# Attention and gated feed-forward on one core: both parts of the weighted sums of a head group issued together

## The chip, the cores and the metric

The kernel runs on one core of a Trainium2 chip. The metric is the device time of one execution in microseconds (us); for the kernel before, three executions were timed. Engines are named as in the profile: PE (matmuls), PEld (its weight loads), DVE (vector engine), ACT (scalar engine), POOL, and SP, which here only issues DMAs.

## The reference

32 sequences of 256 tokens with 128 features pass through attention with 16 heads of 8 features, a residual and a layer norm, then a gated feed-forward net with a hidden width of 512, a residual and a layer norm.

```python
scores = jnp.einsum('bhid,bhjd->bhij', Q, K) / jnp.sqrt(jnp.float32(hd))
delta = t[:, None] - t[None, :]
decay = jnp.where(delta < 0, 0.0, -delta.astype(jnp.float32))
scores = jnp.where(delta < 0, -jnp.inf, scores) + decay
out = jnp.einsum('bhij,bhjd->bhid', softmax(scores), V)      # then @ Wo.T + bo
x = layernorm(x + attention)

h = silu(x @ w1.T * s1) * (x @ w2.T * s2)
h = gelu(h @ h1.T * sh1)
h = gelu(h @ h2.T * sh2)
x = layernorm(x + h @ w3.T * s3)
```

Everything is float32. The entries of the five weight matrices are small whole numbers times a scale per output.

## The kernel before

**Pairs and steps.** Two sequences (512 tokens) form a pair; there are 16 pairs, 0 to 15. `step(n)` (L713) does the attention weights of pair n. Woven into it are the row maxima of pair n+1, the projections of pair n+2, the end of the feed-forward net of pair n-2, and, in the second half of the step, the feed-forward net of pair n-1 (`feed`, L558).

**Places.** The first half of a step is a loop over twelve places, i = 0 to 11 (L721). The 16 heads are four groups of four, and each group owns three places. At the first two of a group, `weigh` (L429) computes scores of two heads for all queries against the first 128 keys; at the third, scores of all four heads for the second 128 keys against the second 128 queries (tiles with a d in the name, s_1d for group 1). ACT takes the exponential of each score tile into a tile e, and POOL puts zeros above the diagonal (L462). At the same place `row_maxima` (L370) computes score tiles of the next pair, PE adds the causal mask to them with four small bf16 matmuls (s<-tri_q,ident_b), and DVE reduces them to maxima m. In the profile a `weigh` tile reads s<-qs,ks (64 rows) and a `row_maxima` tile s<-ks,qs (62 rows).

**Score tiles in PSUM.** `two` (L288) gives tiles of two banks from a pool of three, used for the scores of `weigh` and `row_maxima` and for the gates and hidden layers. A tile can be written again when its reader (ACT's exponential, DVE's reduction, a gate's product) is done. `work` (L285) gives tiles of one bank from a pool of two.

**Weighted sums.** `outputs(n, a)` (L469) is a generator for group a: 16 matmul records over 256 columns (jc = 0, first 128 keys) and 16 over 128 columns (jc = 1, second 128 keys) accumulate into the tile pa, in packets of four for the four column strips of the array. pa takes two groups; after the second group ACT copies it to oT, PE transposes it (pt), and DVE divides by the sums (rec, on). Each `next` of the generator runs it to its next `yield`. It is made at the third place of its group, so its first `next` comes at the first place of the next group: jc = 0 at places 3, 6 and 9, jc = 1 at 4, 7 and 10, each behind the place's score tiles (L728), and oT at 7, the transposition at 8. After `outputs` of a place come, by place, a transposition of the normed x of pair n-1 (px1T, place 9) or a part of the projections (pxT at 1, pq at 3, pk at 5, each of which ACT and DVE split into a high and a low half: qhi, qlo, khi, klo).

**Gates.** The fourth group's generator runs in the second half. `feed` yields after each of its four gates: a gate is four matmuls into one tile (pw), a SiLU on ACT (sg), a product on DVE (h0w), its rounded copy (a CAST, h) and the rest as a low half, which POOL computes for the first two gates and DVE for the other two. At each yield `rest` (L749) takes one step: before the change the first three are jc = 0, then jc = 1 with oT, then the transposition; the fourth runs the transposition of the maxima (pm) and the division. Then come two hidden layers (podd, peven), whose matmuls take the halves of h in the order of the gates.

**Order.** PE, DVE, ACT and SP keep the order in which the program calls them (`InOrder`, L50); nothing is reordered by cost. The pools decide only which tile a new one takes, and so what it waits for.

Of the kernel before, what the change touches and what calls it, by code (L numbers as in the profile page):

```python
# [33 lines left out]
G, C = 4, 4  # L34
# [27 lines left out]
def tile_attn_ffn(  # L62
# [96 lines left out]
    def prepare(func):  # L159

        act.activation(nothing, half[:, 0:1], func)
# [123 lines left out]
    def work(nm):  # L285
        return ps_w.tile([P, 512], F32, name=nm, tag="work")
# [179 lines left out]
        es.append(e)  # L466


    def outputs(n, a):  # L469
        v = pairs[n]["v"]  # L470
        *first, second = pairs[n][("e", a)]
        r, e = divmod(a, 2)
        if e == 0:
            pairs[n]["pa"] = work(f"pa_{n}_{r}").rearrange("c (b i) -> c b i", b=2)
        pa = pairs[n]["pa"]
        for jc in range(2):
            for b in range(2):
                for c in range(C):
                    h, p = c // 2, c % 2
                    at = VSLOT * (C * r + c) + VHEAD * e  # L480
                    pe.matmul(
                        pa[32 * c : 32 * (c + 1), b, jc * P :],
                        lhsT=v[:, 2 * b + jc, at : at + 32],
                        rhs=second[:, p, h, b, :] if jc else first[h][:, p, b, :],
                        start=(e == b == jc == 0), stop=(e == b == jc == 1),
                        tile_position=(0, 32 * c),
                    )
            if jc == 0:
                yield
        if e == 0:  # L490
            return
        oT = op.tile([P, TOK], F32, name=f"oT_{n}_{r}", tag="oT", bufs=1)
        act.copy(oT, pa.rearrange("c b i -> c (b i)"))
        yield

        if r == 0:
            pairs[n]["on"] = op.tile([P, NT, D], F32, name=f"on_{n}", tag="on", bufs=1)
        on = pairs[n]["on"].rearrange("i t (r e c d) -> i t r e c d", r=2, e=2, c=C)
        po = work(f"pt_{n}_{r}").rearrange("i (t c k) -> i t c k", t=NT, c=C)
        for t in range(NT):  # L500
            pe.transpose(po[:, t].rearrange("i c k -> i (c k)"), oT[:, t * P : (t + 1) * P], ident)
        yield
        rec = mp.tile([P, NT, C, 2], F32, name=f"rec_{n}_{r}", tag="rec")
        vec.reciprocal(rec, po[:, :, :, HD : HD + VHEAD + 1 : VHEAD])
        for e in range(2):
            vec.tensor_tensor(
                on[:, :, r, e], po[:, :, :, VHEAD * e : VHEAD * e + HD],
                rec[:, :, :, e : e + 1].to_broadcast([P, NT, C, HD]), ALU.mult,
            )
# [19 lines left out]
    def first_norm(n):  # L529
        x1 = x1s[n % 3]  # L530
        yield from layernorm(pairs[n]["xb"], x1, f"a_{n}")
        pairs[n] = dict(x1=x1)
# [4 lines left out]
    def turn(n, exact):  # L537
        pt = work(f"px1T_{n}")
        for t in range(NT):
            pe.transpose(pt[:, t * P : (t + 1) * P], pairs[n]["x1"][:, t, :], ident)  # L540
        x1T = xtp.tile([P, 2, TOK], F32R, name=f"x1T_{n}", tag="x1T")
        if exact:
            act.copy(x1T[:, 0, :], pt)
            vec.tensor_tensor(x1T[:, 1, :], pt, x1T[:, 0, :].bitcast(F32), ALU.subtract)
        else:
            x1T = x1T.bitcast(F32)
            vec.tensor_copy(x1T[:, 0, :], pt)
        pairs[n]["x1T"] = x1T
# [72 lines left out]
    def inexact_weights():  # L621

        found = const.tile([P, 11], F32, name="found")
        at = 0
        for nm, *_ in layers:
            rows = [t[nm].rearrange("p k o -> p (k o)") for t in (loaded, near)]
            for c in range(0, rows[0].shape[1], HID):
                whole, part = (t[:, c : c + HID] for t in rows)
                act.copy(part, whole)
                differ = once.tile([P, HID], F32, name=f"differ_{at}", tag="differ")  # L630
                vec.scalar_tensor_tensor(
                    differ, whole, 1.0, part.bitcast(F32), ALU.mult, ALU.not_equal,
                    accum_out=found[:, at : at + 1],
                )
                at += 1
                yield
        ones_col = const.tile([P, 1], F32, name="ones_col")
        nc.gpsimd.memset(ones_col, 1.0)
        count = work("pcount")
        pe.matmul(count[0:1, 0:11], lhsT=ones_col, rhs=found, start=True, stop=True)  # L640
        total = const.tile([1, 1], F32, name="total")
        vec.tensor_reduce(total, count[0:1, 0:11], AX.X, ALU.add)
        number = const.tile([1, 1], I32, name="number")
        vec.tensor_copy(number, total)
        pairs["inexact"] = number

    def last(n, exact, ws, gp):
        h = pairs[n]["h"]
        pT = work(f"pw3_{n}")
        for k in range(KC):  # L650
            parts = [h[:, i, k, :] for i in range(2 if exact else 1)]
            product(pT, ws["w3"][:, k, :], parts, k == 0, k == KC - 1)
        yT = gp.tile([P, TOK], F32, name=f"yT_{n}", tag="sg")
        act.activation(yT, pT, AF.Copy, scale=sc["s3"])
        yield
        po = work(f"py_{n}").rearrange("p (t d) -> p t d", d=D)
        for t in range(NT):
            pe.transpose(po[:, t, :], yT[:, t * P : (t + 1) * P], ident)
        y = yp.tile([P, NT, D], F32, name=f"y2_{n}", tag="y")
        vec.tensor_tensor(y, po, pairs[n]["x1"], ALU.add)  # L660
        z = yp.tile([P, NT, D], F32, name=f"z_{n}", tag="z")
        yield
        yield from layernorm(y, z, f"f_{n}")
        sp.dma_start(out=ov[n], in_=z)
        del pairs[n]

    def run(gen):
        for _ in gen:
            pass
# [43 lines left out]
    def step(n, exact=None, ws=None, hp=None, gp=None):  # L713


        side = iter(())
        settling = (
            last(n - 2, exact, ws, gp) if n > 1 else first_norm(0) if n else inexact_weights()
        )
        ahead = project(n + 2) if n + 2 < NPAIR else iter(())  # L720
        for i in range(3 * G):  # L721
            weigh(n, i)
            j = i + {0: LEAD, 1: -LAG}.get(n, 0)
            if n + 1 < NPAIR and 0 <= j < 3 * G:
                row_maxima(n + 1, j)
            if i == 3 and late:
                run(late.pop())
            next(side, None)  # L728
            if n and i == 9:
                turn(n - 1, exact)  # L730
            if i in ((0, 2) if n > 1 else (0, 2, 4, 6)) if n else i < 11:
                next(settling, None)

            if i in ((3, 4, 5) if n == 1 else (1, 3, 5)):
                next(ahead, None)
            if i % 3 == 2:
                run(side)
                side = outputs(n, i // 3)
            if n == 0 and i == 3 * G - LEAD:
                maxima_to_rows(1)  # L740
        if n < 2:
            run(settling)
        run(ahead)
        if n + 2 < NPAIR:
            stack(n + 2, "q")
            stack(n + 2, "k", sp if n else act)


        def rest():  # L749
            for _ in range(3):  # L750
                next(side)
                yield
            if n == 1:
                for i in range(3 * G - LAG, 3 * G):
                    row_maxima(2, i)
                    yield
            if 0 < n < NPAIR - 1:
                maxima_to_rows(n + 1)
            run(side)
            yield  # L760
            if n + 2 < NPAIR:
                project_values(n + 2)
                yield
            last_steps = finish(n)
            next(last_steps)
            yield
            yield from last_steps
            if n:
                yield
                yield from first_norm(n)  # L770
            if n == NPAIR - 1:
                yield
                turn(n, exact)
            if n > 1:
                next(settling)
                late.append(settling)

        if n:
            prepare(AF.Silu)
        due = rest()  # L780
        for _ in feed(n - 1, exact, ws, hp, gp) if n else ():
            next(due, None)
        run(due)
# [84 lines left out]
```

## Time and profile before

| | |
|---|---|
| three timed executions | 823.65, 823.84, 826.28 us; median 823.84 |
| the profiled execution | 828.74 us |
| its span, first to last instruction | 826.8 us |
| mean granted PE clock | 0.969 |
| instructions | 17426 |
| PE, groups over pa | 1024 matmul records over the 256-column tiles, 379 ns median; 4 x 256 over 128 columns, 273 ns |

The page gives the busy time of each engine and the chain of work that ended last. Matmul records overlap, so their durations are longer than their distance in time: how long a group holds PE is read from start to start. In the chain the lengths of neighbouring groups add up to time. A single engine's timeline gives the start, the length and, in brackets, the idle time before it with what ended it. In a list of stretches the columns after the length are the busy times of the engines with their numbers of instructions, then the granted PE clock, the share of the DMA engines, and GB/s.

Steps 2 to 13 repeat alike, one every 47.4 us; step 8 lies between 418 and 465 us. PE's clock was granted at half in stretches within the first 100 us and at the very end.

### The profile page before, as it was taken

The numbers are of one execution on the slowest core, as the hardware profiler recorded it, in microseconds if no ns is written. First come the engines' busy times: TensorE is split into PE (matmuls) and PEld (weight loads), VectorE is DVE, ScalarE is ACT, GpSimd is POOL, SyncE is SP. The second block draws the span as 40 slices with busy tenths as digits, with TensorE's granted clock in tenths as the row PEclk, the third lists the DMA queues.
The fourth block names the chain that finished last, engine by engine and source line by source line (L and its number), as shares of the span: only waits on it lengthen the run. The fifth ranks groups of instructions, "written<-read, shape, count | busy, mean of one in ns | idle before, by whom it ended". The sixth has DMA issues, their size and how long they took to land.

```text
span 826.8 us, 17426 instructions
## 1 busy us (share of the span) xinstructions
PE 788.6 (95%) x7046; PEld 556.4 (67%) x7046; DVE 636.0 (77%) x1245; ACT 527.3 (64%) x719; POOL 259.7 (31%) x340
## 2 busy tenths in 40 slices
PE   5896999999999999999999999999999999999994
PEld 2564576676767667676767767676776767666673
DVE  6786677778888887878888777878888787873674
ACT  5065465766576666667677676657666666758662
POOL 5033322414242432314233341423234242424210
PEclk9569699999999999999999999999999999999998
DMA  6814040311404040230404031040404023000001
GB/s 146 224 49 106 14 104 16 91 29 36 97 14 106 27 103 17 61 72 14 106 27 106 14 90 43 20 111 16 107 26 103 5 52 68 14 4 13 1 13 31
DMA packets 39882, 47.49 MB, mean 57 GB/s; under 512 B 3952, under 2 KB 21616, under 8 KB 39792
## 3 DMA queue, kind: packets, MB, share of 16 engines
q1 hardware_dynamic: 37136, 42.82, 21.7%
q10 hardware_dynamic: 2656, 3.48, 1.9%
q8 instruction: 57, 0.93, 0.5%
q14 instruction: 33, 0.27, 0.1%
HBM read 7.48 MB, written 4.19 MB: 14 GB/s over the span
## 4 chain that ended last, share of the span: by engine, by line
PE 83%; DVE 4%; ACT 3%; issue 1%; DMA 1%; POOL 0%; SPq 0%; ACTq 0%; POOLq 0%; DVEq 0%
PE peven L58 14%; PE podd L58 13%; PE s L58 12%; PE pa L58 11%; PE pw L58 10%; PE s_0d L58 2%; PE s_2d L58 2%; PE s_3d L58 2%; PE s_1d L58 2%; PE po L58 2%; PE pq L58 2%; PE pk L58 2%; PE pt L58 2%; PE pv L58 2%; PE px1T L58 1%; PE py L58 1%
## 5 line engine op out<-in xcount | busy, mean ns | idle before, releaser
L58 DVE TENSOR_REDUCE m<-s 128x4 f32<-128x1024 f32 x128 | 155.6, 1219 | 15.8 <-PE s L58 14.6
L58 ACT ACTIVATE e<-s 128x1024 f32<-128x1024 f32 x128 | 130.7, 1022 | 45.6 <-PE s L58 36.2
L462 POOL TENSOR_SCALAR_AFFINE_SELECT e<-e 128x512 f32<-128x512 f32 x128 | 82.3, 643 | 220.9 <-ACT e L58 192.1
L58 PE MATMUL podd<-h,h_near 128*128 128x512 f32 x512 | 131.4, 403 | 1.0 <-DVE m L58 0.5
L58 PE MATMUL peven<-hodd,h_near 128*128 128x512 f32 x512 | 122.7, 396 | 0.0
L58 PEld LDWEIGHTS peven<-hodd,h_near 128*128 128x128 f32 x512 | 95.7, 187 | 23.4 <-DVE hodd L58 0.3
L58 PEld LDWEIGHTS podd<-h,h_near 128*128 128x128 f32 x512 | 91.7, 188 | 23.2 <-DVE h L58 3.5
L58 ACT ACTIVATE hodd<-podd,sh 128x512 fp32r<-128x512 f32 x64 | 44.0, 688 | 62.9 <-PE podd L58 62.8
L58 PE MATMUL pw<-x1T,w_near 128*128 128x512 f32 x256 | 75.6, 418 | 1.1 <-DVE h0w L58 1.1
L58 PEld LDWEIGHTS s<-qs,ks 64*128 64x128 f32 x512 | 39.3, 190 | 49.3 <-issue 35.8
L273 POOL TENSOR_TENSOR rsa<-rsa,half 128x4 f32<-128x4 f32 x16 | 16.3, 1017 | 176.0 <-DVE rsa L58 176.0
L58 PE MATMUL pa<-e,vaug 128*32 128x256 f32 x1024 | 71.4, 393 | 0.0
L58 DVE SCALAR_TENSOR_TENSOR h0w<-pw,s,sg 128x512 f32<-128x512 f32 x64 | 47.9, 749 | 29.4 <-ACT sg L58 29.4
L58 PE MATMUL s<-qs,ks 64*128 64x256 f32 x512 | 65.8, 337 | 0.7 <-ACT e L58 0.5
L58 DVE TENSOR_TENSOR heven<-evenw,heven 128x512 fp32r<-128x512 f32 x64 | 44.2, 692 | 26.6 <-ACT evenw L58 26.1
L58 ACT ACT_TABLE_LOAD x47 | 60.3, 1283 | 3.4 <-issue 2.6
L58 ACT ACTIVATE sg<-pw,s 128x512 f32<-128x512 f32 x64 | 43.6, 683 | 28.3 <-PE pw L58 27.9
L58 PE MATMUL s<-ks,qs 62*128 62x256 f32 x512 | 57.3, 303 | 3.6 <-ACT e L58 2.4
L58 ACT ACTIVATE heven<-peven,sh 128x512 fp32r<-128x512 f32 x48 | 33.4, 695 | 39.8 <-PE peven L58 39.8
L58 PEld LDWEIGHTS pw<-x1T,w_near 128*128 128x128 f32 x256 | 43.4, 188 | 18.4 <-ACT nothing L58 5.8
L580 POOL TENSOR_TENSOR h<-h0w,h 128x512 fp32r<-128x512 f32 x31 | 40.0, 1290 | 43.5 <-DVE h L58 41.3
L58 DVE TENSOR_TENSOR hodd<-oddw,hodd 128x512 fp32r<-128x512 f32 x64 | 43.8, 684 | 10.9 <-ACT oddw L58 10.8
(147 smaller groups left out, 1418.7 us busy)
## 6 DMA issues: line engine op xcount, KB each, us to landing
qs<-qhi SPq DMA_DIRECT2D x32, 256.0 KB
qs<-qlo SPq DMA_DIRECT2D x32, 256.0 KB
ks<-khi SPq DMA_DIRECT2D x26, 256.0 KB
ks<-klo SPq DMA_DIRECT2D x26, 256.0 KB
x<-in_x_dram SPq DMA_DIRECT2D x16, 256.0 KB
out_dram<-z SPq DMA_DIRECT2D x16, 256.0 KB
ks<-khi ACTq DMA_DIRECT2D x6, 256.0 KB
ks<-klo ACTq DMA_DIRECT2D x6, 256.0 KB
```

What stands on the lines that cost most here:

```text
L58: return lambda *args, **kw: self.tc.keep_in_program_order(call(*args, **kw))
L273: nc.gpsimd.tensor_tensor(rs, rs, half, ALU.pow)
L462: nc.gpsimd.affine_select(out=on_diagonal, in_=on_diagonal, pattern=[[0, on_diagonal.shape[1]], [1, P]], base=0, channel_multiplier=-1, co ...
L580: (nc.gpsimd if o < (1 if final else 2) else vec).tensor_tensor(h[:, 1, o, :], whole, h[:, 0, o, :].bitcast(F32), ALU.subtract)
```

## The change

`outputs` now yields before any matmul instead of between the two parts, so at places 3, 6 and 9 it does nothing, and at 4, 7 and 10 both parts follow each other. For the fourth group (`at_once`) it doesn't yield there: both parts and the copy to oT come between the first two gates, the transposition between the second and the third, and nothing between the third and the fourth. `rest` takes an empty step in its place, so all that follows keeps its yield. pa is still taken from its pool at the first `next`.

```diff
-    def outputs(n, a):
+    def outputs(n, a, at_once=False):
         ...
             pairs[n]["pa"] = work(f"pa_{n}_{r}").rearrange("c (b i) -> c b i", b=2)
         pa = pairs[n]["pa"]
+        if not at_once:
+            yield
         for jc in range(2):
             for b in range(2):
                 for c in range(C):
         ...
-            if jc == 0:
-                yield
         if e == 0:
             return
         oT = op.tile([P, TOK], F32, name=f"oT_{n}_{r}", tag="oT", bufs=1)
         act.copy(oT, pa.rearrange("c b i -> c (b i)"))
         yield
         ...
                 run(side)
-                side = outputs(n, i // 3)
+                side = outputs(n, i // 3, at_once=i == 3 * G - 1)
         ...
         def rest():
-            for _ in range(3):
+            for _ in range(2):
                 next(side)
                 yield
+            yield
             if n == 1:
```

In the order of PE's instructions of a step, places 3, 6 and 9 lose the 256-column group, which stands at 4, 7 and 10 ahead of the 128-column one; pq, the score tiles of place 7 and px1T come directly behind the masks of places 3, 6 and 9. Among the gates the order becomes pw, both parts, pw, pt, pw, pw, pm. On ACT the copy to oT of the fourth group comes ahead of the SiLU of the second gate. DVE, POOL and SP keep their order.

## The prediction

> **What bounds the kernel now.** I read the page first (busy shares and the chain), then a table by stages, then the chain in order of time through one step of the pair loop, then single engines in the places that the change touches. All times are from the one profiled execution.
>
> ```profile
> PE 788.6 (95%) x7046; PEld 556.4 (67%) x7046; DVE 636.0 (77%) x1245; ACT 527.3 (64%) x719; POOL 259.7 (31%) x340
> ...
> PE 83%; DVE 4%; ACT 3%; issue 1%; DMA 1%; POOL 0%; SPq 0%; ACTq 0%; POOLq 0%; DVEq 0%
> ```
>
> ```profile
> 388.00:436.00 48.00, 48.00 (x450) 34.40 (x448) 38.63 (x76) 32.81 (x45) 15.67 (x20) 1.00 0.24 58
> 436.00:484.00 48.00, 48.00 (x449) 34.33 (x448) 38.95 (x76) 32.27 (x45) 16.11 (x21) 1.00 0.24 57
> ```
>
> In the second view the columns are the stretch, its length, then busy time of PE, PEld, DVE, ACT and POOL, the granted clock, and DMA. PE is busy in 48.00 of 48.00 us at full clock from about 148 to 676 us. A step lasts 47.4 us (the khi instructions of successive steps start at 383.742 and 431.135). So every tenth of a microsecond that PE gains or loses in a step counts whole, twelve times over in steps 2 to 13, which repeat to a few nanoseconds. The four other steps are priced apart.
>
> The chain through places 5 to 8 of step 8 (start, length, work):
>
> ```profile
> 428.77 1.27 PE s_1d L58 x20
> 430.04 1.06 PE pk L58 x2
> 431.10 0.85 PE s L58 x12
> 431.95 1.00 PE pa L58 x16
> 432.95 0.85 PE s L58 x12
> 433.81 0.57 PE pa L58 x16
> 434.38 1.27 PE s_2d L58 x20
> ```
>
> Here the 1.00 us of pa stands between the two score blocks of places 6 and 7. Beside it ACT runs, 0.07 us earlier on the clock of the timeline:
>
> ```profile
> 431.13 0.69 ACT L58 ACTIVATE khi<-pk,bk_sb 128x512 fp32r<-128x512 f32 x1 [0.62 <-PE pk L58]
> 431.72 1.02 ACT L58 ACTIVATE e<-s 128x1024 f32<-128x1024 f32 x1
> ```
>
> **The change part by part.** Nothing is added or removed: the same 32 matmul records of each group of four heads (16 over 256 columns, 16 over 128) are issued together. DVE, POOL and SP (and with SP the DMAs) keep their order; on ACT one copy moves (below). Three effects, all on PE.
>
> (1) Places 3/4 and 9/10: one interruption less. Inside the 256-column group the packets of four start 0.216 us apart; the last is followed 0.329 us later by whatever comes next, so leaving costs 0.113. The first packet of the 128-column group takes 0.133 where the next take 0.109, so entering costs 0.024. Joined, the two parts save 0.137. What then follows the masking matmuls (pq at place 3, px1T at 9) starts as it does elsewhere: mask to pxT takes 0.171 and mask to pa 0.170, and a transposition group takes 0.586 after mask and after pa alike. I take −0.137 twice. Bounds: 0, if joining saves nothing, and −0.17, the whole mask step. Waits checked: px1T asks for nothing new, pq waits only for xT, copied by 423.9. The row maxima of place 10 wait for the exponential of place 9, which ends at 437.794; their weight load would be due at 437.83 and can start 0.05 after that end, at 437.84: the cover has run out but costs 0.01.
>
> (2) Places 6/7: a wait takes the place of the cover. The score tiles rotate through three PSUM buffers; the row maxima of place 7 reuse the tile that the exponential of place 6 reads. Before, pa's 1.00 us hid that. Now the block of place 7 starts at 431.88 and its row maxima are due 0.34 later, at 432.22. The exponential still ends at 432.737, since it starts only when khi leaves ACT (0.585 after khi's start, in each of the twelve steps). What such a wait costs is shown at place 1 of every step:
>
> ```profile
> 420.25 1.01 ACT L58 ACTIVATE e<-s 128x1024 f32<-128x1024 f32 x1
> ...
> 421.31 0.30 PEld L58 LDWEIGHTS s<-ks,qs 62*128 62x128 f32 x4
> 421.31 0.50 PE L58 MATMUL s<-ks,qs 62*128 62x256 f32 x4
> ...
> 421.74 0.11 PEld L58 LDWEIGHTS <-ident_b 64*64 64x64 bf16 x4
> ```
>
> The exponential ends at 421.26; the weight load follows 0.05 later and the maxima take 0.43 to the mask instead of 0.33, because the weights too waited. So at place 7: maxima at 432.79, mask 433.22, pa 433.40, both parts 0.888 + 0.550, and s_2d at 434.84 where it stood at 434.309: +0.53 with the saved interruption in it. Behind the wait stand mask, both pa parts and all of place 8, PE being in order. Bounds: +0.43 (no slower restart) and +0.65 (the whole cover of 1.00 lost less the slack of 0.35 that the block itself gives).
>
> The Trainium skill, "TensorE: Matmul & The Clock Gate", Part 3, The mechanism, has PE pull weight loads ahead of matmuls in flight. By it the restart would cost no extra 0.10 and the twelve steps 1.2 us less; the row above, where the load itself waits, decides.
>
> (3) The gates: pa's second part now precedes the second gate (pw1) instead of following it. PE alone would save: two pw groups of 1.13 and 1.03 lose their seams with pa, and podd would start at 447.53, not 447.86 (−0.33). But the gate's chain gets later. sg of gate 1 starts 0.04 after its last matmul ends, so at 445.10 (was 444.66), now behind the oT copy on ACT, which has ended by 444.61 and hides. From there, on DVE, before:
>
> ```profile
> 445.38 0.75 DVE L58 SCALAR_TENSOR_TENSOR h0w<-pw,s,sg 128x512 f32<-128x512 f32 x1 [0.23 <-ACT sg L58]
> 446.17 0.64 DVE L58 CAST h<-h0w 128x512 fp32r<-128x512 f32 x1
> 447.14 0.75 DVE L58 SCALAR_TENSOR_TENSOR h0w<-pw,s,sg 128x512 f32<-128x512 f32 x1 [0.33 <-ACT sg L58]
> 447.92 0.54 DVE L58 CAST h<-h0w 128x512 fp32r<-128x512 f32 x1
> ...
> 450.35 0.69 DVE L58 TENSOR_TENSOR h<-h0w,h 128x512 fp32r<-128x512 f32 x1
> ```
>
> ```profile
> 451.09 0.30 PEld L58 LDWEIGHTS podd<-h,h_near 128*128 128x128 f32 x2 [0.16 <-DVE h L58]
> ```
>
> The last low part of h ends at 451.038 and podd's load for it starts 0.05 later; it already waits 0.16 there, which its prefetch just covers. After the change: h0w of gate 1 at 445.82, its cast at 446.60 to 447.03 (free of POOL, 0.43), POOL's low part 447.12 to 448.40. Gate 2 ends 0.10 later than before (pw2 from 445.25), so its h0w runs 447.24 to 447.99 and its cast would start at 448.02, under POOL. In all 31 casts that overlap a POOL low part, the cast ends 0.28 after POOL does (446.81 against 446.53 here): so 448.69, was 448.46. The rest follows in the old spacing: last low part to 451.27, load at 451.32, +0.23. PE's early start is thus swallowed in podd, and the step is +0.23 later, not −0.33. Bounds: −0.01 (the cast unhindered) and +0.35 (restart 0.10 slower once more). I take +0.23 by the 31 casts.
>
> A step: −0.137 − 0.137 + 0.53 + 0.23 = +0.48; twelve of them +5.8 us.
>
> The other steps, from their own rows. Step 0 is bound by DVE and then by the ACT queue's DMA issues before oT (72.85): 0, bounds ±0.5. Step 1, partly at half clock (granted 0.66 over 80 to 100): exponential of place 6 ends 96.95, maxima due 96.59, so +0.38 there, −0.25 and −0.14 elsewhere, +0.23 in the gates: +0.2. Step 14 has no pq and pk: without pq the wait comes at place 4 too (exponential of place 3 ends 710.15, maxima due 709.77, s_1d 0.39 later) and what follows carries it: +0.6. Step 15 has no row maxima, so nothing can wait for their tile, exponentials start earlier: −0.5. Sum +0.3.
>
> In all +6.1 us on a profiled execution of 828.74 (span 826.8), so 834.8 there. That execution is 4.9 above the median of the three timed, 823.84; the steady steps being the same in kind, I add the 6.1 to the median: 829.9. The noise bound I use for no change is 0.3%, 2.5 us.
>
> The Trainium skill, "TensorEngine Tiling (Array Packing)", Tiling Modes, Key Properties, says that a change of tiling mode drains TensorE. The seams of 0.113 above are such changes, and the rule alone favours the change. With the some 175 ns of drain that "TensorE: Matmul & The Clock Gate" gives under Single matmul latency, an estimate by it for four joints in 16 steps is 11 us less, 812.6.
>
> **The rivals.**
> - No new wait binds: PE simply loses its seams, three times 0.137 and 0.33 at the gates, 0.74 a step; over some 13 steps −9.7 us, 814. For it: PE's 83% of the chain. Against it: the exponential of place 6 would have to end by 432.17, 0.56 earlier than it does, and podd's load already waits for DVE.
> - Only the gates turn out well (the cast escapes POOL, or podd's load is not last): −0.27 + 0.53 − 0.33 = −0.08 a step, −1.0 in all and 0.3 for the other steps: 823.1, no change. It decides from a cast of gate 2 that ends before 448.1.
> - A rotation of the two work buffers puts pq behind DVE's add of the previous tile (to 425.75; due at 425.22) and px1T behind the division of heads (to 437.71; due at 437.02): +0.58 and +0.75 a step more, 847. The waits written in the new instruction streams name other producers, so little speaks for it.
>
> **How the numbers follow.** The forecast, +4 to +8 us: 0.78. Only the gates turn out well: 0.11. No wait binds: 0.06. The buffers: 0.05. Summing the lower bounds of the forecast's own terms (−0.17 twice, +0.43, −0.01: +0.08 a step) gives +1, the upper ones (0, +0.65, +0.35: +1.0) +12, but ends on one side together are unlikely. The range 823.0 to 833.5 takes in the second case and the bulk of the first. Faster by over 0.3%: the 0.06 and 0.02 of the second case. Within: 0.09 of the second and 0.03 of the first case's low end. Slower: the remaining 0.80.
>
> **What would show it.** Step length from khi to khi 47.88 instead of 47.40. At place 7 the maxima (s<-ks,qs) start 0.05 after the exponential of place 6 ends, and take 0.43. The two pa groups of 1.00 and 0.57 become one of about 1.44. At the gates, podd's weight load waits for DVE twice, some 0.4 us each time, and the second of these loads starts 10.25 us after the start of s_3d's mask (441.07) instead of 10.02. I am wrong if ACT's exponential moves (khi gone from before it), if pa splits again on POOL's masking of e_3d (it ends 442.975, due by 443.1), or if the half-clock stretches of the first 100 us (20.5 us up to 54.9, 13.7 us up to 95.9) change their length.

## The result, and the profile after

The changed kernel takes 830.88 us (median of six executions, 830.1 to 832.75) beside 823.81 for the kernel before (six executions, 823.39 to 826.28). The ratio is 1.0081 with a 95% interval of 1.0063 to 1.0098: slower by 7.07 us, and the forecast was 829.9, 6.1 slower.

The profiled execution took 831.62 us with a span of 829.9. It stands only 2.9 above the profiled execution of before, because that one was later from the start: khi of step 2 began at 146.73 there and at 143.42 here, and between 80 and 100 us PE ran at half clock for 13.7 us there and for 3.4 us here (last section). So the two traces are compared from khi of step 2 on: from there to the end before took 680.07 us (826.80 − 146.73) and after takes 686.47 (829.89 − 143.42), **+6.40**.

The page's busy times and the shares of the chain of work that ended last:

```profile
PE 784.8 (95%) x7046; PEld 562.2 (68%) x7046; DVE 629.4 (76%) x1245; ACT 525.3 (63%) x719; POOL 259.7 (31%) x340
...
PE 80%; ACT 6%; DVE 3%; issue 1%; POOL 1%; DMA 0%; ACTq 0%; POOLq 0%; DVEq 0%
```

The list of stretches in the steady part (stretch, length, busy time of PE, PEld, DVE, ACT, POOL, granted clock, DMA share, GB/s):

```profile
388.00:436.00 48.00, 47.59 (x443) 34.47 (x443) 38.03 (x76) 32.17 (x45) 15.66 (x20) 1.00 0.25 58
436.00:484.00 48.00, 47.59 (x444) 34.48 (x442) 38.05 (x76) 32.16 (x45) 15.67 (x20) 1.00 0.24 57
```

PE had been busy in 48.00 of 48.00 us. Now 0.41 us in each stretch is idle at a clock still granted in full, and ACT has grown from 3% to 6% of the chain. One hole a step has opened, and its releaser is on ACT. The chain in order of time shows it, in step 8 again (start, length, work):

```profile
430.18 1.10 POOL e_1d L462
431.28 0.04 issue
431.32 1.02 ACT e L58
432.35 0.04 issue
432.39 0.68 PE s L58 x8
433.07 1.44 PE pa L58 x32
434.51 1.27 PE s_2d L58 x20
```

Before, this stretch was PE from end to end. Now the chain leaves PE and passes through the exponential of place 6. PE's timeline at the same place:

```profile
431.48 0.50 PE L58 MATMUL s<-qs,ks 64*128 64x256 f32 x4
432.39 0.50 PE L58 MATMUL s<-ks,qs 62*128 62x256 f32 x4 [0.41 <-ACT e L58]
432.82 0.25 PE L58 MATMUL s<-tri_q,ident_b 64*64 64x128 bf16 x4
433.00 1.07 PE L58 MATMUL pa<-e,vaug 128*32 128x256 f32 x16
433.89 0.62 PE L58 MATMUL pa<-e_1d,vaug 128*32 128x128 f32 x16
434.44 0.66 PE L58 MATMUL s_2d<-qs,ks 64*128 64x128 f32 x8
```

The row maxima of place 7 (432.39) follow the score tile of place 7 by 0.91 us, where 0.34 is the undisturbed distance, and wait 0.41 for the exponential of place 6, which ends at 432.34. Both pa parts stand behind them, at 433.00, and s_2d at 434.44 starts 3.707 after khi (430.735) instead of 3.174. The list of waits on PE has this kind at 6.3 us over 16 waits; before it was 3.0 over 2.

The steady step is 47.887 us from khi to khi (mean of eleven, 47.868 to 47.901), where it was 47.398: +0.489. By parts, each the distance between two starts on PE, and beside it the change that the prediction gave:

| from, to | before | after | change | predicted |
|---|---|---|---|---|
| khi to s_2d (places 6, 7) | 3.174 | 3.707 | +0.53 | +0.53 |
| s_2d to the first gate (9, 10) | 6.99 | 6.86 | −0.13 | −0.137 |
| first gate to podd | 6.58 | 6.26 | −0.32 | −0.33 |
| podd to pv | 3.81 | 4.35 | +0.54 | (+0.23 with the line above) |
| pv to the next khi (3, 4) | 26.84 | 26.71 | −0.13 | −0.137 |

The gates, on DVE, as in the rows of before (in brackets the idle time before an instruction, and its releaser):

```profile
445.82 0.75 DVE L58 SCALAR_TENSOR_TENSOR h0w<-pw,s,sg 128x512 f32<-128x512 f32 x1 [0.67 <-ACT sg L58]
446.61 0.43 DVE L58 CAST h<-h0w 128x512 fp32r<-128x512 f32 x1
447.26 0.75 DVE L58 SCALAR_TENSOR_TENSOR h0w<-pw,s,sg 128x512 f32<-128x512 f32 x1 [0.23 <-ACT sg L58]
448.05 0.64 DVE L58 CAST h<-h0w 128x512 fp32r<-128x512 f32 x1
...
450.57 0.69 DVE L58 TENSOR_TENSOR h<-h0w,h 128x512 fp32r<-128x512 f32 x1
```

On POOL the low part of gate 1, and in PE's weight loads what waits for the last two halves of h:

```profile
447.12 1.29 POOL L580 TENSOR_TENSOR h<-h0w,h 128x512 fp32r<-128x512 f32 x1 [0.58 <-DVE h L58]
```

```profile
450.59 0.30 PEld L58 LDWEIGHTS podd<-h,h_near 128*128 128x128 f32 x2 [0.43 <-DVE h L58]
451.32 0.30 PEld L58 LDWEIGHTS podd<-h,h_near 128*128 128x128 f32 x2 [0.43 <-DVE h L58]
```

The cast of gate 2 (448.05) runs under POOL's low part and ends at 448.69, 0.28 after POOL does; the last low part ends at 451.26 and podd's load follows at 451.32. PE reaches podd 0.32 us earlier, and waits there twice.

### The profile page after: what moved, and what is told of

The parts are those of the page before. It is cut to its first block, busy times and chain, and to the rows that moved or that the text cites. A ratio compares the mean times of both kernels' runs of the same rounds, so it can differ in the third digit from the quotient of the medians.

```text
span 829.9 us, 17426 instructions
## 1 busy us (share of the span) xinstructions
PE 784.8 (95%) x7046; PEld 562.2 (68%) x7046; DVE 629.4 (76%) x1245; ACT 525.3 (63%) x719; POOL 259.7 (31%) x340
## 4 chain that ended last, share of the span: by engine, by line
PE 80%; ACT 6%; DVE 3%; issue 1%; POOL 1%; DMA 0%; ACTq 0%; POOLq 0%; DVEq 0%
PE podd L58 14%; PE peven L58 14%; PE pa L58 10%; PE pw L58 10%; PE s L58 10%; ACT e L58 2%; PE s_2d L58 2%; PE s_3d L58 2%; PE po L58 2%; PE s_0d L58 2%; PE pt L58 2%; PE s_1d L58 2%; PE pq L58 2%; PE pv L58 2%; PE pk L58 1%
## 5 line engine op out<-in xcount | busy, mean ns | idle before, releaser
L58 ACT ACTIVATE e<-s 128x1024 f32<-128x1024 f32 x128 | 128.9, 1022 | 29.5 <-PE s L58 29.4
L58 PE MATMUL podd<-h,h_near 128*128 128x512 f32 x512 | 138.1, 408 | 1.1 <-DVE m L58 0.5
L58 PE MATMUL pw<-x1T,w_near 128*128 128x512 f32 x256 | 71.8, 413 | 1.1 <-DVE h0w L58 1.1
L58 PEld LDWEIGHTS pw<-x1T,w_near 128*128 128x128 f32 x256 | 44.5, 188 | 13.7 <-PE pa L58 2.0
L58 PEld LDWEIGHTS s<-ks,qs 62*128 62x128 f32 x512 | 41.4, 197 | 15.8 <-ACT e L58 8.8
```

What stands on the lines that cost most here:

```text
L58: return lambda *args, **kw: self.tc.keep_in_program_order(call(*args, **kw))
```

## The experiments

The theory after the result: the change is four separate ones. Joining groups 0 and 2 (places 3/4, 9/10) is a gain of 0.13 each. Joining group 1 (places 6/7) uncovers the exponential of place 6 and costs 0.53. Joining the fourth group ahead of the second gate saves PE 0.32 and loses 0.54 to h. The rivals: that the two halves act on each other, that the order matters in itself and not the cover, and that the gates' loss comes from the joining and not from the place between the gates. All experiments use the same two switches in `outputs`; where only `joined` or `late` is named, the other is off:

```diff
-    def outputs(n, a):
+    def outputs(n, a, late=False, joined=False):
...
+        if late:
+            yield
         for jc in range(2):
...
-            if jc == 0:
+            if jc == 0 and not (late or joined):
                 yield
```

### The places alone, and the gates alone

The first run moves groups 0 to 2 as the change does and leaves the gates as they were:

```diff
-                side = outputs(n, i // 3)
+                side = outputs(n, i // 3, late=i < 3 * G - 1)
```

> Only the three joints among the score tiles; the fourth group stays split between the first three gates as before. Step length from khi to khi, 47.40 before and 47.89 in the changed kernel. Theory (two joints gain 0.14 each, the one at place 7 pays 0.53 for the exponential of place 6, the gates pay 0.22): step 47.66, whole kernel +3.2 us on 823.8, 827. Rival A (joining itself costs, 0.12 at each of the four joints): 47.77, +4.7. Rival B (all of the loss is in the gates, the places only gain 0.14 each): 46.99, -5.

The second has only the fourth group as the change has it:

```diff
-                side = outputs(n, i // 3)
+                side = outputs(n, i // 3, joined=i == 3 * G - 1)
...
-            for _ in range(3):
+            for _ in range(2):
                 next(side)
                 yield
+            yield
```

> Only the joint between the first two gates; places 3 to 10 stay split as before. Theory: step 47.62 (+0.22), podd starts 0.32 earlier after the first gate and its load for the last low part of h comes 0.22 later; +3.0 us, 827. Rival A (0.12 for each joint): 47.52, +1.6. Rival B (all in the gates): 48.3, +11.

Measured: the places alone give a step of 47.673 (+0.275) and 828.38 us, ratio 1.0053 [1.0036, 1.0069]; the gates alone 47.622 (+0.224) and 828.47, 1.0052 [1.0032, 1.0071]. The sum of the two, +0.499, is the changed kernel's +0.489. Both parts are losses by themselves and they don't act on each other.

### Without the group that uncovers the exponential

Only groups 0 and 2 are joined late; group 1 and the fourth stay as before:

```diff
-                side = outputs(n, i // 3)
+                side = outputs(n, i // 3, late=i in (2, 8))
```

> Only groups 0 and 2 joined, at places 4 and 10; group 1 and the fourth group split as before. Theory: two seams fewer and no new wait in steps 2 to 13, step 47.13 (-0.27), -3.5 us, 820.3, faster than both kernels. In step 14, which has no projections, the wait on the exponential of place 3 appears at place 4 and costs 0.4. Rival A (joining itself costs 0.12): 47.64, +2.9. Rival C (pa later is pa too late: what reads it moves): 47.4 to 47.6.

Measured: 47.137 and 820.3 us, ratio 0.9958 [0.9944, 0.9972]. It beats both kernels. Each of the two joints is worth 0.13 us a step ((47.398 − 47.137) / 2), and group 1 alone costs 0.536 (47.673 − 47.137). PE's timeline at places 6 and 7 of one step, where the 256-column part of pa stands again ahead of the scores of place 7:

```profile
333.09 1.07 PE L58 MATMUL pa<-e,vaug 128*32 128x256 f32 x16
334.09 0.51 PE L58 MATMUL s<-qs,ks 64*128 64x256 f32 x4
334.43 0.40 PE L58 MATMUL s<-ks,qs 62*128 62x256 f32 x4
334.76 0.25 PE L58 MATMUL s<-tri_q,ident_b 64*64 64x128 bf16 x4
334.94 0.65 PE L58 MATMUL pa<-e_1d,vaug 128*32 128x128 f32 x16
```

The maxima follow the scores by 0.34, with no wait.

### Joined, but with cover

Is it the joining of group 1 that costs, or only that nothing stands ahead of the row maxima of place 7? Here all three groups are joined late, and at place 7 the outputs come between the scores and the row maxima:

```diff
             weigh(n, i)
             j = i + {0: LEAD, 1: -LAG}.get(n, 0)
+            if i == 7:
+                next(side)
             if n + 1 < NPAIR and 0 <= j < 3 * G:
                 row_maxima(n + 1, j)
...
-            next(side, None)
+            if i != 7:
+                next(side, None)
...
-                side = outputs(n, i // 3)
+                side = outputs(n, i // 3, late=i < 3 * G - 1)
```

> Like e1 (all three groups joined, gates as before), but at place 7 both parts are issued ahead of the row maxima of that place instead of behind them, so that they cover the exponential of place 6. Theory: the wait of 0.53 goes; instead the score block of place 7 is cut in two, which adds two changes between the shapes of matmuls, 0.09 and 0.10 by the rows of before, against 0.14 saved: +0.05 there; step 47.40 - 0.27 + 0.05 = 47.18, -2.9 us, 820.9. Rival A (joining itself costs): 47.77 as in e1. Rival C (pa later is too late): 47.66 as in e1, since pa ends no earlier.

Measured: 47.194 and 821.48 us, ratio 0.9967 [0.9955, 0.9978]. The wait is gone from PE's timeline:

```profile
333.18 0.50 PE L58 MATMUL s<-qs,ks 64*128 64x256 f32 x4
333.61 1.07 PE L58 MATMUL pa<-e,vaug 128*32 128x256 f32 x16
334.50 0.62 PE L58 MATMUL pa<-e_1d,vaug 128*32 128x128 f32 x16
335.05 0.50 PE L58 MATMUL s<-ks,qs 62*128 62x256 f32 x4
335.48 0.25 PE L58 MATMUL s<-tri_q,ident_b 64*64 64x128 bf16 x4
```

The weight load of these maxima, and the exponentials of places 6 and 7, which follow each other on ACT:

```profile
335.05 0.30 PEld L58 LDWEIGHTS s<-ks,qs 62*128 62x128 f32 x4 [0.20 <-ACT e L58]
```

```profile
333.02 1.93 ACT L58 ACTIVATE e<-s 128x1024 f32<-128x1024 f32 x2
```

Both exponentials have ended by 334.95, 0.10 before the load, so it isn't they that hold it. The joint stays, and 0.48 of the 0.54 comes back. What costs is the order against the reader of the PSUM tile. Over leaving group 1 split it brings nothing, though: from the mask of place 6 to s_2d it is 2.66 us here (333.00 to 335.66), and 2.60 there (332.91 to 335.51). The joint's 0.13 is spent again: scores to pa take 0.43, where scores to maxima take 0.34, and the maxima 0.43 to their mask, where it was 0.33. Why these two are longer was not tested. But 0.43 is also what the maxima take after their wait in the changed kernel, so that figure goes with maxima that don't follow their scores directly, with a wait or without.

### Joined one place early

Now both parts of groups 0 to 2 come at places 3, 6 and 9, where the first part was, so the second part and all that follows it in the generator come a place earlier:

```diff
-                side = outputs(n, i // 3)
+                side = outputs(n, i // 3, joined=i < 3 * G - 1)
```

> Groups 0 to 2 joined early instead of late: both parts at places 3, 6 and 9 (the transposition pt follows at place 7); the fourth group split as before. The same seams are saved as in e1. Theory (a joint costs what the score block left without cover must wait for): at place 7 no wait, since pa and pt stand around it, -0.14; at place 5 the row maxima of s_1d wait for the exponential of place 4, which khi's sister qhi and pq now delay, +0.35; at place 11 those of s_3d wait for the exponential of place 10, which stands behind the copy x1T, +0.26; step 47.87, +6 us, 830. Rival A (joining costs by itself): 47.77. Rival C (only lateness costs): 47.40 - 0.41 = 46.99, -5.

Measured: 48.179 and 838.57 us, ratio 1.016 [1.014, 1.0179]: slower as expected, but by 0.31 a step more. The expectation overlooked that the transposition pt moves as well, from place 8 to place 7. Then nothing stands between places 8 and 9, and the row maxima of place 9 wait for the exponential of place 8, in PE's timeline:

```profile
336.49 0.66 PE L58 MATMUL s_1d<-ks,qs 62*128 62x128 f32 x8 [0.25 <-ACT e L58]
...
343.37 0.50 PE L58 MATMUL s<-qs,ks 64*128 64x256 f32 x4
343.94 0.50 PE L58 MATMUL s<-ks,qs 62*128 62x256 f32 x4
344.37 0.25 PE L58 MATMUL s<-tri_q,ident_b 64*64 64x128 bf16 x4
```

The weight load of the maxima of place 9:

```profile
343.94 0.30 PEld L58 LDWEIGHTS s<-ks,qs 62*128 62x128 f32 x4 [0.27 <-ACT e_2d L58]
```

From the scores to the maxima it is 0.57 instead of 0.34, and 0.43 instead of 0.33 to the mask, 0.33 in all, about the miss. The first row is a wait of the same kind at place 5 (0.25, in twelve steps), and there is one at place 11 (0.17 in this step); both were expected.

This run also settles something that the chain of the changed kernel leaves open. There the exponential of place 6 starts 0.04 after POOL's mask of e_1d ends, so the chain goes back to POOL; the prediction said that ACT's khi holds it. Here, on ACT and on POOL:

```profile
338.47 0.69 ACT L58 ACTIVATE khi<-pk,bk_sb 128x512 fp32r<-128x512 f32 x1 [1.11 <-PE pk L58]
339.06 1.01 ACT L58 ACTIVATE e<-s 128x1024 f32<-128x1024 f32 x1
```

```profile
337.43 1.09 POOL L462 TENSOR_SCALAR_AFFINE_SELECT e_1d<-e_1d 128x1024 f32<-128x1024 f32 x1 [0.24 <-ACT e_1d L58]
```

POOL ends at 338.52, 0.54 ahead, and the exponential still starts 0.585 after khi's start, as in every kernel traced (0.585 to 0.589). Its own scores don't hold it either: in the changed kernel it starts 0.69 after their first matmul (430.63), and where an exponential waited for its scores alone it was 0.55 to 0.60 (places 3 and 9 of that step). It is khi; the chain's step to POOL is a coincidence in time.

### The fourth group behind the second gate

Joined, but with both parts after the second gate, so that the second gate's chain to h isn't delayed:

```diff
-                side = outputs(n, i // 3)
+                side = outputs(n, i // 3, joined=i == 3 * G - 1)
...
-            for _ in range(3):
+            yield
+            for _ in range(2):
                 next(side)
                 yield
```

> Only the fourth group joined, as in e2, but both parts stand between the second and the third gate instead of the first and the second, so the SiLU of the second gate is not late. Theory: PE reaches podd 0.3 earlier as in e2, but DVE's chain through the casts and low parts is held by POOL's low part of gate 0 and ends where it ended before: the gain is waited away, step 47.40 (0.00, bounds -0.05 and +0.05), 823.8. Rival (the loss of e2 comes from joining, not from the late second SiLU): 47.62 as in e2. Rival (the chain has slack): 47.08, -3.9 us.

Measured: 47.396 and 823.93 us, ratio 0.9995 [0.9986, 1.0005], no change at all. PE again reaches podd 0.32 earlier (6.257 after the first gate, where it was 6.58), and the loads give it back:

```profile
351.42 0.30 PEld L58 LDWEIGHTS podd<-h,h_near 128*128 128x128 f32 x2 [0.21 <-DVE h L58]
352.14 0.30 PEld L58 LDWEIGHTS podd<-h,h_near 128*128 128x128 f32 x2 [0.43 <-DVE h L58]
```

So the place between the gates costs 0.224 (the run with the gates alone), and the joining itself is worth nothing, since DVE's last half of h sets when podd can go on.

With groups 0 and 2 added:

```diff
-                side = outputs(n, i // 3)
+                side = outputs(n, i // 3, late=i in (2, 8), joined=i == 3 * G - 1)
```

> e3 (groups 0 and 2 joined late) together with e6 (the fourth group joined behind the second gate); group 1 split as before. Theory: 47.14 + 0.00, like e3, 820.3. Rival (the chain has slack): 46.82, 816.5.

Measured: 47.133 and 821.62 us, 0.9962 [0.9949, 0.9974], the same as without the fourth group.

### Can the wait for h be filled?

The last four matmuls of podd_0/1 wait for the two halves of h of the fourth gate. Two matmuls of a later product, which need only h of the first gate, could run in front of them. Three kernels take them from podd_2, the next product; on top of the run above, of the kernel before, and of the changed kernel:

```diff
             for os in ((0, 1), (2,), (3,)):
-                both = two(f"p{nm}_{n}_{os[0]}")
-                ph = {o: both[:, o - os[0], :] for o in os}
-                for k in range(KC):
+                if nm == "odd" and os == (0, 1):
+                    columns(os, (0, 1, 2))
+                    columns((2,), (0,))
+                    columns(os, (3,))
+                else:
+                    columns(os, range(1 if nm == "odd" and os == (2,) else 0, KC))
```

(`columns(os, ks)` takes the tile at its first call and issues the matmuls of the hidden blocks ks.)

> e7 (groups 0, 2 and the fourth joined, no new wait), and in the first hidden layer the first two matmuls (0.46 us) of the third column block are issued ahead of the last four of the first two blocks, which are the ones that wait for the last halves of h. Theory (the seams saved at the gates are waited away there): the wait of 0.33 is filled with work that came later, step 47.13 - 0.33 = 46.80, -7.5 us on 823.8, 816.5, and podd's loads wait no more. Rival (PE gains nothing at the gates because the seams come back elsewhere): 47.13, 820.

> The kernel before with the same two matmuls moved, nothing else. Theory: before, PE arrives just in time for the last half of h, so there is nothing to fill: 47.40 (0.00), 823.8. Rival (the move gains by itself): 47.07.

> The changed kernel with the same two matmuls moved. Theory: its wait on the last half of h is 0.33 + 0.23 = 0.56 a step, of which 0.46 are filled: step 47.89 - 0.46 = 47.43; the wait at place 7 stays. About 825. Rival (the 0.22 at the gates is not a wait on h): 47.89.

All three missed. Steps: 47.176 (on the run above; 820.63 us, 0.9955 [0.994, 0.9969]), 47.769 (on before; 829.71, 1.006 [1.0042, 1.0078]) and 47.907 (on after; 831.71, 1.0084 [1.0067, 1.0101]). The last is near the number of its rival, that the loss at the gates is no wait on h. But from podd to pv it takes 4.35 us as in the changed kernel, with two matmuls more in between: the wait was there, and 0.46 of it was filled. In the first, podd's loads wait for h only four times in the whole run (1.3 us; 31 times and 10.7 us without the two matmuls), yet nothing is gained. DVE's and then PEld's timeline of the first, from the products on. pv is the product that gives V of a later pair and vaug its copy with the bias; hodd is the result of the first hidden layer; pon is the transposition of the divided sums, onT its copy, and po their product with Wo:

```profile
355.80 0.89 DVE L58 TENSOR_TENSOR vaug<-pv,bv_sb 128x128 f32<-128x128 f32 x4 [0.53 <-PE pv L58]
356.61 0.68 DVE L58 TENSOR_TENSOR hodd<-oddw,hodd 128x512 fp32r<-128x512 f32 x1
357.20 0.69 DVE L58 COPY onT<-pon 128x512 f32<-128x512 f32 x1
```

```profile
355.93 1.23 PEld L58 LDWEIGHTS podd<-h,h_near 128*128 128x128 f32 x6
357.94 0.97 PEld L58 LDWEIGHTS po<-wo_sb,onT 128*128 128x128 f32 x8 [0.78 <-DVE onT L58]
```

podd_2 stands between pon and po, and po needs onT, which DVE makes from pon behind vaug and a half of hodd: from the start of pv (354.71) to the load of po it is 3.23 us, though PE has 0.46 us less to do in between. Eight matmuls of podd_2 fill that stretch (it is 3.34 in the run above, whose pv takes 0.10 longer; the load of po waits 0.30 there, which its prefetch covers); six leave a hole. In the trace as a whole the load or matmul of po waits for onT 32 times, 20.7 us, where it was 20 times and 10.9 us. On the kernel before, where podd hardly waited for h, pv starts 0.47 later and the shorter podd_2 gives nothing back: from pv to the even products 6.09 us instead of 6.19, so +0.37 for a mere change of order. All three have the 32 waits at po.

If that is the cause, the two matmuls have to come from podd_3, behind po:

```diff
-                    columns((2,), (0,))
+                    columns((3,), (0,))
...
-                    columns(os, range(1 if nm == "odd" and os == (2,) else 0, KC))
+                    columns(os, range(1 if nm == "odd" and os == (3,) else 0, KC))
```

> e7 (groups 0 and 2 late, the fourth group behind the second gate; step 47.13) with the first two matmuls of the FOURTH odd product (podd_3, behind po) issued ahead of the last four of podd_0/1, where e8 took the first two of the third (podd_2, between pon and po). Theory A (e8 and e9 lost the gain because the chain pv, vaug, hodd, onT on VectorE takes 3.24 us from the start of pv to the load of po, which e7 already fills, so that a shorter podd_2 only turned into a wait of po on onT): pv to po is 3.34 as in e7, podd_3 is shorter by 0.46, pv starts 0.15 later than in e7 (20.56 as in e8), so the step is 47.13 - 0.46 + 0.15 = 46.82, and 14 steps of it 4.3 us: about 817. The waits of po on onT are 20 and 11 us in sum as in e7, not 32 and 21. Rival B (the hoisted matmuls cost about what they save wherever they come from, or the next stage, the even products, waits for hodd instead): step 47.13 to 47.20, 820 to 821, as e8.

Measured: 46.717 and 816.91 us, ratio 0.9914 [0.9892, 0.9936], the fastest of the study. PEld of the same part of a step:

```profile
352.23 1.70 PEld L58 LDWEIGHTS podd<-h,h_near 128*128 128x128 f32 x8
354.24 0.97 PEld L58 LDWEIGHTS po<-wo_sb,onT 128*128 128x128 f32 x8 [0.31 <-DVE onT L58]
355.13 1.24 PEld L58 LDWEIGHTS podd<-h,h_near 128*128 128x128 f32 x6
```

po stands 3.23 behind pv as in the kernel with podd_2, and now the shorter product comes after it: from pv to the even products 5.63 us, against 6.09 there. The step is 0.10 better than expected, because pv's load hardly waits any more for mlo, the low half of the transposed maxima on DVE (0.29 in twelve steps of the run without these two matmuls, two waits in this one) and pv takes 0.89 instead of 1.00; the expectation had kept that.

Last, the fourth group is split again as in the kernel before, the rest stays. If the 0.32 that PE saves by the joining was only swallowed by the wait for h, it must show now:

```diff
-                side = outputs(n, i // 3, late=i in (2, 8), joined=i == 3 * G - 1)
+                side = outputs(n, i // 3, late=i in (2, 8))
...
-            yield
-            for _ in range(2):
+            for _ in range(3):
                 next(side)
                 yield
```

> e11 with the fourth head group issued as in the kernel before (first part behind the first gate, second part behind the second); groups 0 and 2 late and the two hoisted matmuls of podd_3 as in e11. In e6 and e7 joining the fourth group started podd 0.32 earlier and brought nothing, because podd's loads then waited for h. Theory A (the 0.32 was real PE time, swallowed only by that wait, which e11 has removed): without the joining podd starts 16.61 after khi instead of 16.285, takes 4.28 to pv in both, so pv at 20.89, even products at 26.52, step 46.715 + 0.32 = 47.04; about 820 on the median of e11's 817 + 14 x 0.32 = 821.4 at most. Rival B (something else absorbs it, as DVE's chain from h to hodd and onT): podd again at 16.61, but step 46.7 to 46.8, about 817.

Measured: 47.037 and 820.14 us, ratio 0.9943 [0.9927, 0.996]. The step is 0.32 longer. Joining the fourth group is worth its 0.32 as soon as podd does not wait for DVE, and nothing while it does.

## Why the prediction was right

It gave +6.1 us and +0.48 for a steady step; measured were +7.07 (5.2 to 8.1 by the interval) and +0.489. It was right by its own steps:

- **(1) One interruption less**, −0.137 twice: −0.13 each in the changed kernel, and −0.13 each in the run with groups 0 and 2 alone. The joined pa takes 1.44 in the chain, as stated. The drain of some 175 ns that the Trainium skill gives for a single matmul in "TensorE: Matmul & The Clock Gate", Single matmul latency, was taken there for such a joint; the runs show 0.13.
- **(2) The wait in place of the cover**, +0.53: measured +0.533 at the same place, for the reason given (the run without group 1, the run with cover and the run one place early each say so), with the maxima 0.05 after the end of the exponential and 0.43 to the mask. The slower restart was the step on which the prediction set a row against a rule. The Trainium skill, "TensorE: Matmul & The Clock Gate", Part 3, The mechanism, has weight loads pulled ahead of matmuls in flight when they go to other row groups or to the background weight buffer. Here the restart cost its extra 0.10, and again at place 9 of the run one place early. The reason given for the 0.10, that the weights too waited, is not shown: in the run with cover the maxima take the same 0.43 and no exponential holds their load.
- **(3) The gates**, +0.23 for −0.33 on PE: measured +0.22 a step and −0.32, with the cast of gate 2 ending 0.28 after POOL, the last low part at 451.26 (given: 451.27) and the load at 451.32 (given: 451.32). The gates alone cost 0.224.
- **The other steps**, +0.3: step 14 +0.72 (given +0.6) and step 15 −0.35 (given −0.5), from py to py. Steps 0 and 1 can't be compared, since the clock differs there; of the 6.40 us from khi of step 2 on, twelve steps of 0.489 are 5.87 and these two 0.37; most of the remaining 0.16 is the gain at places 3/4 of step 2, which lies ahead of that khi. Steps 14 and 15 were both given too low, by 0.27 together, and no row here checks the +0.2 for step 1. The 0.7 between 6.40 and the medians' 7.07 lies within the interval.
- **The rivals**: that no new wait binds would have needed an earlier exponential of place 6, and the chain now runs through it. A good end at the gates alone would have needed a cast before 448.1; it ended at 448.69. No wait on a work buffer appears.
- **A sign of being wrong that did appear:** the half-clock stretches of the first 100 us changed their length. The prediction named two of before, 20.5 and 13.7 us; a third lay between 20 and 31 us, where the granted clock was 0.54. In the changed kernel there are 20.5 and 3.4 us. The profiled execution missed its 834.8 us by 3.2, with a start that was 3.3 shorter up to khi of step 2. The steady step is untouched by this, since its clock was granted in full in both kernels. The prediction put its sum on the median of before without an argument that the starts average out; that the medians agree with it to 1.0 us is in part luck.

What the prediction did not see is outside its sum. It took the four joints as one change; only two of them had to be made for a gain of 0.4%, and the joint of the fourth group was worth 0.32 a step behind a wait which it named itself (podd's load) and which could be filled.

## What to carry to other kernels

An interruption on a saturated engine has two sides: what leaving and entering cost (0.13 us here), and what the work in it covers. Before moving work out of a place, list for every tile in a rotation whose reader is still at work when its next writer is due, and move only what covers no reader (two of the four joints here). And when PE's time saved in one place ends in a wait, look for independent work to fill it, but take that work from behind the next wait, not from the cover in front of it: two matmuls brought nothing when they were taken from the product ahead of po, and 0.42 us a step when they were taken from the one behind it.

## What was not expected of the hardware

The start is not the same in the traces, though the kernels differ only in the order of the work. PE's half-clock stretches in the first 100 us differ in multiples of 3.4 us: between 70 and 100 us it is 13.7 us in the profiled execution of before, 3.4 in that of after, and 6.8 in that of the fastest kernel. There is one trace of each kernel, so part of that could come from the edits; but the mean granted clock of the executions of before alone goes from 0.966 to 0.984. The list of stretches over the first 100 us, of before and then of after (the granted clock is the third column from the end):

```profile
0.00:100.00 100.00, 78.65 (x675) 48.30 (x676) 70.85 (x120) 44.04 (x53) 32.57 (x58) 0.78 0.45 111
```

```profile
0.00:100.00 100.00, 78.16 (x710) 49.97 (x714) 72.68 (x125) 46.02 (x56) 34.21 (x60) 0.88 0.45 111
```

With these starts khi of step 2 came at 146.73 and at 143.42, 3.3 us apart, half of what the change is worth; how much of that is the clock's was not separated. The steady steps repeat to some hundredths of a microsecond in every kernel. For a change of this size the length of the steady step tells more than two spans do.
